# Layer 0's attention by head pairs instead of by halves: both halves' scores, then both halves' values, and all softmax sums through DRAM

## The chip, the cores and the metric

The kernel runs on one core of a Trainium2 chip. The metric is the device time of one launch in microseconds (us). A core has TensorE (PE in the profile; its weight loads are PEld), VectorE (DVE), ScalarE (ACT), GpSimd (POOL) and SyncE (SP, which issues DMAs). PSUM has eight banks, which hold the matmuls' results.

## The reference, cut to what matters

Eight images of 32×32 pixels with 384 channels go through two attention layers and a feed-forward network. What the change touches is layer 0's attention, with six heads of 64 channels and a position term:

```python
attn = einsum('bqd,bkd->bqk', q * SCALE, k)
attn = attn.reshape(b * NH, h, w, h, w) + rel_h[:, :, :, :, None] + rel_w[:, :, :, None, :]
attn = softmax(attn.reshape(b * NH, hw, hw), axis=-1)
out = einsum('bqk,bkd->bqd', attn, v)
...
x = x + (out @ proj_w + proj_b)
```

Each image has hw = 1024 tokens, so each head has 1024×1024 scores. Then follow layer 1 (one head of 384 channels, causal in blocks of 256 tokens) and, for five images, the feed-forward network.

## The kernel before, in words

**The images.** They run one after the other in the order 5, 0, 1, 2, 3, 4, 6, 7 (`ORDER`). An image's layer 0 is followed by its layer 1, and so on; products for the next image are placed among them. TensorE's order within the attention is fixed by hand: every matmul is issued after the one named in `last_matmul`. The other engines take their instructions in the order in which the program text issues them, unless `behind_of` or `tc.issue_after` puts one behind another. [...]

**The attention of one image** (`attend0_fast`). Six heads make three pairs p (`NPAIR`), 1024 queries make two halves of 512, 1024 keys make eight blocks c (`NJ`). A pair's two heads use the two halves of TensorE's rows or columns.

- `scores(p, c, half)`: for both heads, keys times queries (L904) and then the position term, a matmul of `unit` with the pair's table `r` (L908), into two PSUM banks. ScalarE takes the exponential of each (L915) into `pr`, 128 keys × (2 heads × 512 queries).
- `add_up`: VectorE adds the eight `pr` to `total`: one addition at L920, six at L922. These are the softmax sums over the blocks, still spread over 128 partitions.
- `values`: 32 passes (L930) of v against the eight `pr`, into one bank `av`. ScalarE copies it to `oT` (L1002).
- `over_tiles`: VectorE transposes the total within 32×32 blocks (L939) and reduces it (L941) to `few`, 128 × 32 numbers.
- `gathered`: SP writes `few` to DRAM (L949) and reads it back in four DMAs (L953) as `parts`, so that each partition has the four parts of its own sums. VectorE then reduces `parts` (L969).
- `reciprocals` with `parts=None`: instead of the DRAM trip TensorE multiplies `few` with `fold` (L964, `den`).
- `widened`: VectorE copies the reciprocals wide (L978) and transposes them (L979). The result scales `oT`: on GpSimd at L999, or on VectorE for an image's last halves (L1012, L1015).
- `later(p + 1)`, which calls `place`: rounds the next pair's position factors (ScalarE L784), subtracts to get the low part (two VectorE subtractions, L794), and sends both through 16 DMAs (L800; eight on SP's queue, eight on GpSimd's) into the `r` that L908 of the next pair reads.
- `residual`: SP loads the image x in four DMAs (L122), GpSimd adds the projection's bias in eight additions (L883). The result is first used when the projection is added.

**The order before.** For each pair and half: eight blocks of scores; the adds; behind the sixth of the seven adds (`adds[5]`) the reciprocals of the half before; the values. `residual` is placed in the first half of pair 1. `later` is placed after the first half of pairs 0 and 1. The sums of an image's last half go through L964. The projection (`pj`, L1021) then starts with tokens 0 to 511, in 24 passes: four token blocks j, three pairs i, two passes each.

**Buffers.** `page` has 12 buffers of 128×1024 floats (each `pr`, `total`, transposed total and wide takes one). `image` has ten larger buffers (q, k, v, `oT`, x, normalised forms, position factors). PSUM has eight banks in one pool.

**The end of the program.** The last image's output leaves in DMAs on SP's queue (L1525). Then a flag, set where a reciprocal or another value was unfit, is loaded, and a branch decides whether a general version of the whole program follows. It does not follow with these inputs.

Of the kernel before, what the change touches and what calls it, by code (L numbers as in the profile page):

```python
# [15 lines left out]
ALU = mybir.AluOpType  # L16
# [3 lines left out]
P = 128  # L20
B, H, W, C = 8, 32, 32, 384
T = H * W
NJ = T // P
NC = C // P
NH, HD = 6, 64
NPAIR = NH // 2
# [8 lines left out]
ORDER = (B_FFN, *range(B_FFN), *range(B_FFN + 1, B))  # L35
AFTER = dict(zip(ORDER, ORDER[1:]))
# [55 lines left out]
def conv_attn_hybrid(  # L92
# [19 lines left out]
    nc = tc.nc  # L112
# [15 lines left out]
    wproj_sb = tile_of("wproj_sb", [P, NC, C])  # L128
# [145 lines left out]
    N_SEEN = B * PER_IMAGE  # L274
    seen = const.tile([P, 2, N_SEEN], F32, name="seen")
    flag = const.tile([1, 1], I32, name="flag")

    def judge_sums(pools):

# [141 lines left out]
    def stages(pools):  # L421
# [98 lines left out]
        def project(w, cols, xT, j, name):  # L520

            ps = pools.o_tile(name)
            for k in range(NC):
                nc.tensor.matmul(ps[:, :C], xT[:, k, ts(j, P)], w[:, k, cols], start=(k == 0), stop=(k == NC - 1))  # L524
            return ps[:, :C]
# [361 lines left out]

        def attend0_fast(residual, b, q, k, r, v, later):


            oT = pools.image(f"oT_{b}")

            rows = (slice(0, HD), slice(HD, P))
            last_exp, last_matmul, last_few = [None], [None], [None]

            def behind_last():
                return tc.issue_after(last_matmul[0]) if last_matmul[0] is not None else contextlib.nullcontext()

            def scores(p, c, half):

                sc = [pools.o_tile(f"s0_{b}_{p}_{c}_{half}_{par}") for par in range(2)]
                with behind_last():
                    for par in range(2):
                        nc.tensor.matmul(  # L904
                            sc[par], k[rows[par], p, ts(c, P)], q[rows[par], p, ts(half, 512)], start=True, stop=False
                        )
                    for par in range(2):
                        last_matmul[0] = nc.tensor.matmul(  # L908
                            sc[par], unit[rows[par], c // 2 % 2].rearrange("i h w -> i (h w)"),
                            r(2 * (c // 4) + c % 2, p)[rows[par], ts(half, 512)], start=False, stop=True,  # L910
                        ).ins
                pr = pools.page(f"pr0_{b}_{p}_{c}_{half}")
                for par in range(2):
                    with behind_of(exp_loaded[0]):
                        last_exp[0] = nc.scalar.activation(pr[:, ts(par, 512)], sc[par], AF.Exp).ins  # L915
                return pr
# [58 lines left out]
            def widened(p, half, rt):  # L975
                room = pools.page(f"wide0_{b}_{p}_{half}")
                wide, rb = room[:, :512], room[:, 512:]
                nc.vector.tensor_copy(wide.rearrange("p (n i) -> p n i", i=32), rt.unsqueeze(2).to_broadcast([P, 16, 32]))  # L978
                nc.vector.transpose(rb, wide)  # L979
                return rb  # L980

            xt, waiting = None, None
            for p, half in itertools.product(range(NPAIR), range(2)):
                t, last = ts(half, 512), (p, half) == (NPAIR - 1, 1)
                prs = [scores(p, c, half) for c in range(NJ)]
                if b == ORDER[0] and (p, half) == (0, 0):
                    with tc.issue_after(last_row[0]):
                        layer1_forms(pools, raw1[0], 1)
                if b == ORDER[0] and (p, half) == (2, 0):
                    signs.append(binarize(pools))  # L990
                    next(signs[0])
                total, adds = add_up(p, half, prs)
                if waiting is not None:
                    p0, t0 = waiting[0], ts(waiting[1], 512)
                    with tc.issue_after(adds[4 if last else 5]):
                        rt = reciprocals(*waiting)
                    if not last:
                        rb = widened(p0, waiting[1], rt)
                        nc.gpsimd.tensor_tensor(oT[:, p0, t0], oT[:, p0, t0], rb, ALU.mult)  # L999
                av = values(p, half, prs)  # L1000
                if not last:
                    nc.scalar.copy(oT[:, p, t], av)  # L1002
                if (p, half) == (1, 0):
                    xt = residual()
                if half == 0 and p + 1 < NPAIR:
                    later(p + 1, last_exp[0], adds[-1])
                few = over_tiles(p, half, total)
                at_once = last or (b == ORDER[0] and p == NPAIR - 1)
                if last:
                    with tc.issue_after(last_few[0]):  # L1010
                        rb = widened(p0, waiting[1], rt)
                    nc.vector.tensor_tensor(oT[:, p0, t0], oT[:, p0, t0], rb, ALU.mult)  # L1012
                waiting = (p, half, few, None if at_once else gathered(p, half, few))
            rb = widened(p, half, reciprocals(*waiting))
            nc.vector.tensor_tensor(oT[:, p, t], av, rb, ALU.mult)  # L1015
            with behind_last():
                begun = {j: pools.o_tile(f"pj_{b}_{j}")[:, :C] for j in range(4)}
# [4 lines left out]
                                begun[j], oT[:, i, ts(j, P)], wproj_sb[:, i, :], start=(i == 0), stop=(i == NC - 1)  # L1022
                            ).ins

            def begin(j):
                begun[j] = project(wproj_sb, slice(0, C), oT, j, f"pj_{b}_{j}")

            def more(j):
                nc.vector.tensor_tensor(xt[:, j, :], begun[j], xt[:, j, :], ALU.add)

            return xt, (begin, more)

        def attend0_general(residual, b, q, k, r, v, later):
            state = {}
# [151 lines left out]
        def attend1_fast(xt, b, q, xT, v, other, start):  # L1186
# [24 lines left out]
            def products(av, j, cs, what):  # L1211
                for c in cs:
                    made = nc.tensor.matmul(av, prs[c][:, ts(j - c, P)], what(c), start=(c == 0), stop=(c == j)).ins  # L1213
                return made
# [5 lines left out]
            def add(j, av):  # L1220
                return nc.vector.scalar_tensor_tensor(
                    xt[:, j, :], av[:, :C], rt[:, j : j + 1], xt[:, j, :], ALU.mult, ALU.add
                ).ins
# [13 lines left out]
            def values_and_flag(j, av7):  # L1237
                av = pools.o_tile(f"av1_{b}_{j}")
                last = products(av[:, :C], j, range(j), lambda c: v[:, c, :C])
                worst, made = judge_sums(pools)  # L1240
                with tc.issue_after(made):
                    add(NJ - 1, av7)
                with tc.issue_after(last):
                    last = judge(pools, worst)
                with tc.issue_after(last):
                    products(av[:, :C], j, (j,), lambda c: v[:, c, :C])
                add(j, av)

            held = None if b in AFTER else 3
# [191 lines left out]
        def run(pools):  # L1441
# [49 lines left out]
            for b in ORDER:  # L1491
                xt, more = layer0(b, gn)

                def between():

                    if b in AFTER:
                        norm = group_norm_T(AFTER[b])
                        with behind_of(queries_ended[0]):
                            made = next(norm)
                        yield made  # L1500
                        for i in range(2):
                            with behind_of(last_score[0]):
                                next(norm, None)
                            yield
                        if pools.fast:
                            xf[AFTER[b]] = image_forms(AFTER[b], made, nc.gpsimd)

                started = []

                def start(gn):  # L1510

                    if b < B_FFN and not started:
                        started.append(ffn(xt, b, gn))
                        next(started[0])

                gn = attention1(xt, more, b, between, start)
                start(gn)
                add = next(started[0]) if started else None

                def finish(*js, b=b, xt=xt, add=add):  # L1520
                    if add:
                        xt = add(js)
                    dst = out[b].rearrange("(j p) c -> p j c", p=P)
                    for j in js[::2]:
                        (nc.gpsimd if b in AFTER else nc.sync).dma_start(  # L1525
                            out=dst[:, j : j + 2, :], in_=xt[:, j : j + 2, :]
                        )

                if b < B_FFN:
                    unfinished.append(finish)  # L1530
                else:
                    finish(*(range(NJ) if b in AFTER else (0, 1, 4, 5, 6, 7, 2, 3)))
# [3 lines left out]
    with ExitStack() as scope:  # L1536
        pools = Pools(scope, tc, "f")
        stages(pools)
    failed = nc.values_load(flag[0:1, 0:1], min_val=0, max_val=P)
    with tc.If(failed > 0), ExitStack() as scope:  # L1540
        stages(Pools(scope, tc, "g"))


# [36 lines left out]
```

## Time and profile before

| what | value |
|---|---|
| median of 3 runs | 2262.02 us (2261.88 to 2262.11) |
| the profiled execution | 2262.38 us, span 2260.7 us |
| granted TensorE clock, mean | 0.999 of full speed |
| TensorE busy | 2251.2 us |
| VectorE busy | 1613.0 us (71%) |
| ScalarE busy | 1208.5 us (53%) |
| GpSimd busy | 526.9 us (23%) |
| L904, L908, L930 (scores, position, values), busy | 399.0, 307.7, 340.2 us |
| L920 and L922 (adds), busy | 63.6 and 366.6 us |
| L915 (exponentials), busy | 412.5 us |

A profiled execution gives a span and, for each engine, the time in which it worked. A line of the timeline reads: start and duration in us, engine, line of the program, operation, output `<-` inputs, shape, number of instructions, and in brackets how long the engine had been idle before and what ended that. A pair of matmuls that overlap is counted in both, so a group's busy time can exceed the time that it takes on the clock. The chain of waits follows the work that ended last back to its start.

### The profile page before, as it was taken

To read this page: it belongs to the slowest core of one execution; us is meant where nothing else is said; L and a number is where in the kernel's file an instruction comes from. 1 tells how busy PE (TensorE), PEld (TensorE's weight loads), DVE (VectorE), ACT (ScalarE), POOL (GpSimd) and SP (SyncE) were. 2 spreads that over 40 slices of the span, in tenths; PEclk is the share of its full clock that TensorE was granted. 3 is DMA by queue.
4 is the path that set the end of the run, shared out by engine and by line. 5 is a ranking of instruction groups with operands and counts; after the bars stand their busy time and mean duration, and the time that the engine had idled before them with its cause. 6 is when DMAs were issued, how large, how long until landed. Compare 5 with 4: busy or idle time off the path is not lost.

```text
span 2260.7 us, 30149 instructions
## 1 busy us (share of the span) xinstructions
PE 2251.2 (100%) x10597; PEld 1380.3 (61%) x10597; DVE 1613.0 (71%) x2746; ACT 1208.5 (53%) x2181; POOL 526.9 (23%) x696
## 2 busy tenths in 40 slices
PE   9999999999999999999999999999999999999998
PEld 4547554768546677547685475874477754755475
DVE  6888578876788548886468884578854778727882
ACT  4654266337664457654477543767444766317541
POOL 7513231230231301313102313013040131221310
PEclk9999999999999999999999999999999999999999
DMA  7520562130730205520318203064102382016200
GB/s 188 158 86 29 162 138 68 49 148 29 155 100 29 84 29 126 129 58 1 112 39 189 56 29 112 24 148 112 30 9 104 71 173 64 7 47 155 55 1 30
DMA packets 182049, 188.50 MB, mean 83 GB/s; under 512 B 138764, under 2 KB 151489, under 8 KB 179073
## 3 DMA queue, kind: packets, MB, share of 16 engines
q1 hardware_dynamic: 163680, 115.80, 21.1%
q0 software_dynamic: 17376, 69.30, 9.8%
q8 instruction: 87, 1.43, 0.3%
q10 hardware_dynamic: 832, 1.38, 0.2%
q14 instruction: 74, 0.60, 0.1%
HBM read 84.52 MB, written 51.56 MB: 60 GB/s over the span
## 4 chain that ended last, share of the span: by engine, by line
PE 99%; DMA 0%; DVE 0%; SPq 0%; issue 0%
PE f_s L904 15%; PE f_av L930 15%; PE f_av L1213 8%; PE f_s L1199 8%; PE f_y L1407 7%; PE f_y L1357 7%; PE f_qk L578 6%; PE f_s L908 4%; PE f_pr_A L578 4%; PE f_pr_B L578 3%; PE f_pj L1021 3%; PE f_pj L524 3%; PE f_rel L578 2%; PE f_pr_1v_A L578 2%; PE f_pr_1q_A L578 2%; PE f_pr_1v_B L578 2%
## 5 line engine op out<-in xcount | busy, mean ns | idle before, releaser
L915 ACT ACTIVATE f_pr<-f_s 128x512 f32<-128x512 f32 x768 | 412.5, 595 | 41.8 <-PE f_s L908 37.1
L904 PE MATMUL f_s<-f_q,f_k 64*128 64x512 f32 x1536 | 399.0, 595 | 0.0
L922 DVE TENSOR_TENSOR f_sum<-f_sum,f_pr 128x1024 f32<-128x1024 f32 x288 | 366.6, 1273 | 25.9
L930 PE MATMUL f_av<-f_pr,f_v 128*64 128x512 f32 x1536 | 340.2, 595 | 0.0
L908 PE MATMUL f_s<-f_r,unit 64*128 64x512 f32 x768 | 307.7, 792 | 0.0
L930 PEld LDWEIGHTS f_av<-f_pr,f_v 128*64 128x64 f32 x1536 | 106.0, 137 | 218.2 <-issue 191.9
L904 PEld LDWEIGHTS f_s<-f_q,f_k 64*128 64x128 f32 x1536 | 145.6, 186 | 124.4 <-issue 66.2
L1199 PE MATMUL f_s<-f_q,f_lnT 128*128 128x512 f32 (+3 forms) x576 | 198.3, 488 | 0.0
L1213 PE MATMUL f_av<-f_v,f_pr 128*128 128x385 f32 (+1 forms) x576 | 195.4, 486 | 0.0
L800 POOL DMA_DIRECT2D f_r<-f_far x192 | 102.0, 534 | 382.0 <-DVE f_far L794 174.4
L1208 ACT ACTIVATE f_pr<-f_s 128x512 f32<-128x512 f32 (+3 forms) x96 | 47.0, 490 | 203.2 <-DVE f_s L1204 160.3
L1213 PEld LDWEIGHTS f_av<-f_v,f_pr 128*128 128x128 f32 x576 | 108.1, 190 | 77.0 <-issue 11.5
L1199 PEld LDWEIGHTS f_s<-f_q,f_lnT 128*128 128x128 f32 x576 | 100.7, 190 | 70.0 <-issue 46.9
L1368 DVE TENSOR_REDUCE am<-f_h 128x1 f32<-128x1024 f32 (+2 forms) x80 | 71.6, 946 | 95.6 <-ACT f_h L1361 95.6
L1361 ACT ACTIVATE f_h<-f_y,biases 128x256 f32<-128x256 f32 x240 | 100.6, 470 | 67.0 <-PE f_y L1357 67.0
L908 PEld LDWEIGHTS f_s<-f_r,unit 64*128 64x128 f32 x768 | 75.0, 187 | 89.9 <-issue 89.4
L578 PE MATMUL f_qk<-f_gnT,wq_sb 128*128 128x512 f32 x288 | 127.9, 595 | 0.0
L1407 PE MATMUL f_y<-f_w2a,f_hilo 128*128 128x384 f32 x640 | 127.2, 341 | 0.0
L1002 ACT COPY f_oT<-f_av 128x512 f32<-128x512 f32 x40 | 23.4, 585 | 190.2 <-PE f_av L930 190.2
L920 DVE TENSOR_TENSOR f_sum<-f_pr,f_pr 128x1024 f32<-128x1024 f32 x48 | 63.6, 1325 | 73.5 <-ACT f_pr L915 73.5
L1407 PEld LDWEIGHTS f_y<-f_w2a,f_hilo 128*128 128x128 f32 x640 | 112.6, 188 | 3.8 <-issue 1.4
L1311 POOL PARTITION_ALL_REDUCE qa<-qg x10 | 3.7, 365 | 459.1 <-DVE qg L1309 459.1
(286 smaller groups left out, 4154.4 us busy)
## 6 DMA issues: line engine op xcount, KB each, us to landing
f_far<-f_far SPq DMA_DIRECT2D x48, 512.0 KB, 5.3
f_r<-f_far SPq DMA_DIRECT2D x192, 128.0 KB, 3.3
f_r<-f_far POOLq DMA_DIRECT2D x192, 128.0 KB, 4.5
f_far<-f_far SPq DMA_DIRECT2D x192, 64.0 KB, 4.6
f_x<-in_x SPq DMA_DIRECT2D x32, 384.0 KB, 4.9
f_gnT<-in_xT SPq DMA_DIRECT2D x21, 512.0 KB, 4.7
f_w1a<-w1s POOLq DMA_DIRECT2D x5, 1536.0 KB, 6.7
f_w2a<-w2s POOLq DMA_DIRECT2D x5, 1536.0 KB, 7.3
```

Of the source, the lines that this page charges most:

```text
L578: last_product[0] = nc.tensor.matmul(*args, **kw).ins
L800: put = (nc.gpsimd if i else nc.sync).dma_start(out=r(part, p).bitcast(F32).rearrange("(m i) t -> i m t", i=4)[2 * i + d], in_=pages[i][ts ...
L904: nc.tensor.matmul(sc[par], k[rows[par], p, ts(c, P)], q[rows[par], p, ts(half, 512)], start=True, stop=False)
L908: last_matmul[0] = nc.tensor.matmul(sc[par], unit[rows[par], c // 2 % 2].rearrange("i h w -> i (h w)"), r(2 * (c // 4) + c % 2, p)[rows[pa ...
L915: last_exp[0] = nc.scalar.activation(pr[:, ts(par, 512)], sc[par], AF.Exp).ins
L922: adds.append(nc.vector.tensor_tensor(total, total, pr, ALU.add).ins)
L930: last_matmul[0] = nc.tensor.matmul(av[ts(par, HD), :], v[:, c, ts(2 * p + par, HD)], pr[:, ts(par, 512)], start=(c == 0), stop=(c == NJ - 1),
L1199: last_score[0] = nc.tensor.matmul(sc[:, lo:], xT[:, c // 4, k, ts(c % 4, P)], q[:, half, k, lo:], start=(k == 0), stop=(k == NC - 1),).ins
L1213: made = nc.tensor.matmul(av, prs[c][:, ts(j - c, P)], what(c), start=(c == 0), stop=(c == j)).ins
L1357: nc.tensor.matmul(ps, w1k[i // 2][:, ts(m, P)], xs[i % 2][:, half, i // 2, :], start=(i == 0), stop=(i == 2 * NC - 1))
L1361: nc.scalar.activation(pairs[i][:, m, :, :], ps[:, ts(i % 2, 256)].rearrange("p (j q) -> p j q", j=2), AF.Identity, bias=b1_sb[:, m : m + 1],)
L1407: nc.tensor.matmul(ps[:, :C], h, w, start=(i == 0), stop=(i == len(products) - 1))
```

## The change

It applies to seven of the eight images, all but the first in `ORDER`. The order of one of these images becomes, for each pair:

- the scores of half 0, whose last six exponentials go to two large `image` buffers (three in each) and whose first two go to pages;
- the reciprocals and widening of both halves of the pair before, and their products on GpSimd; `behind_of(last_wide[0])` puts the first add of this pair behind the last widening;
- the adds of half 0; the scores of half 1; the adds of half 1;
- in the last pair, `residual`;
- the values of half 0 and of half 1, each followed by its copy to `oT`;
- `later(p + 1)`, now behind the last add of half 1;
- both halves' transposes and reductions, each followed by its trip through DRAM, in the last pair too, so the matmul of L964 is not used.

After the last pair come the reciprocals of both halves and their products on VectorE, and then the projection in the order j = 0 to 3, each with i = 0, 1, 2. `oT` is taken from its pool after the first values of the image rather than at the start.

At the end of the program the flag is loaded before the last layer 1 addition, and the last output DMA goes to ScalarE's queue instead of SP's.

```diff
-            def scores(p, c, half):
+            def scores(p, c, half, pr=None):
...
-                pr = pools.page(f"pr0_{b}_{p}_{c}_{half}")
+                pr = pools.page(f"pr0_{b}_{p}_{c}_{half}") if pr is None else pr
...
-                nc.vector.transpose(rb, wide)
+                last_wide[0] = nc.vector.transpose(rb, wide).ins
                 return rb
+
+            def by_pairs():
+
+                oT, waiting = None, []
+                for p in range(NPAIR):
+                    last = p == NPAIR - 1
+                    rooms = [pools.flat(f"pr0_{b}_{p}_{i}") for i in range(2)]
+                    prs = [[scores(p, c, 0, rooms[(c - 2) // 3][:, ts((c - 2) % 3, T)] if c > 1 else None) for c in range(NJ)]]
+                    for p0, half, few, parts in waiting:
+                        with behind_of(last_few[0]):
+                            rb = widened(p0, half, reciprocals(p0, half, few, parts))
+                        t = ts(half, 512)
+                        nc.gpsimd.tensor_tensor(oT[:, p0, t], oT[:, p0, t], rb, ALU.mult)
+                    waiting = []
+                    with behind_of(last_wide[0]):
+                        sums = [add_up(p, 0, prs[0])]
+                    prs.append([scores(p, c, 1) for c in range(NJ)])
+                    sums.append(add_up(p, 1, prs[1]))
+                    if last:
+                        xt = residual()
+                    for half in range(2):
+                        av = values(p, half, prs[half])
+                        if oT is None:
+                            oT = pools.image(f"oT_{b}")
+                        if not (last and half):
+                            nc.scalar.copy(oT[:, p, ts(half, 512)], av)
+                    if not last:
+                        later(p + 1, last_exp[0], sums[1][1][-1])
+                    for half in range(2):
+                        with behind_of(last_few[0] if half else sums[1][1][-1]):
+                            few = over_tiles(p, half, sums[half][0])
+                        waiting.append((p, half, few, gathered(p, half, few)))
+                with behind_of(last_few[0]):
+                    for p, half, few, parts in waiting:
+                        t = ts(half, 512)
+                        rb = widened(p, half, reciprocals(p, half, few, parts))
+                        nc.vector.tensor_tensor(oT[:, p, t], av if half else oT[:, p, t], rb, ALU.mult)
+                begun = {}
+                with behind_last():
+                    for j in range(4):
+                        begun[j] = pools.o_tile(f"pj_{b}_{j}")[:, :C]
+                        for i in range(NC):
...
+            if b != ORDER[0]:
+                return rest_of(*by_pairs())
...
+                failed.append(nc.values_load(flag[0:1, 0:1], min_val=0, max_val=P))
                 add(j, av)
...
-                            (nc.gpsimd if b in AFTER else nc.sync).dma_start(
+                            (nc.gpsimd if b in AFTER else nc.scalar if j == js[-2] else nc.sync).dma_start(
...
-    failed = nc.values_load(flag[0:1, 0:1], min_val=0, max_val=P)
-    with tc.If(failed > 0), ExitStack() as scope:
+    with tc.If(failed[0] > 0), ExitStack() as scope:
```

More of the change, by code (lines that the diff above doesn't have):

```diff
@@ L276, in conv_attn_hybrid @@
     flag = const.tile([1, 1], I32, name="flag")
+    failed = []
     def judge_sums(pools):
@@ L888, in attend0_fast @@
         def attend0_fast(residual, b, q, k, r, v, later):
-            oT = pools.image(f"oT_{b}")
             rows = (slice(0, HD), slice(HD, P))
-            last_exp, last_matmul, last_few = [None], [None], [None]
+            last_exp, last_matmul, last_few, last_wide = [None], [None], [None], [None]
             def behind_last():
                 return tc.issue_after(last_matmul[0]) if last_matmul[0] is not None else contextlib.nullcontext()
-            def scores(p, c, half):
+            def scores(p, c, half, pr=None):
                 sc = [pools.o_tile(f"s0_{b}_{p}_{c}_{half}_{par}") for par in range(2)]
@@ L978, in widened @@
                 nc.vector.tensor_copy(wide.rearrange("p (n i) -> p n i", i=32), rt.unsqueeze(2).to_broadcast([P, 16, 32]))
-                nc.vector.transpose(rb, wide)
+                last_wide[0] = nc.vector.transpose(rb, wide).ins
                 return rb
+            def by_pairs():
[38 more added lines that the diff above has]
+                        for i in range(NC):
+                            with tc.issue_after(last_matmul[0]):
+                                last_matmul[0] = nc.tensor.matmul(
+                                    begun[j], oT[:, i, ts(j, P)], wproj_sb[:, i, :], start=(i == 0), stop=(i == NC - 1)
+                                ).ins
+                return xt, oT, begun
@@ L982, in attend0_fast, with rest_of, begin, more @@
+            def rest_of(xt, oT, begun):
+                def begin(j):
+                    begun[j] = project(wproj_sb, slice(0, C), oT, j, f"pj_{b}_{j}")
+                def more(j):
+                    nc.vector.tensor_tensor(xt[:, j, :], begun[j], xt[:, j, :], ALU.add)
+                return xt, (begin, more)
+            if b != ORDER[0]:
+                return rest_of(*by_pairs())
+            oT = pools.image(f"oT_{b}")
             xt, waiting = None, None
@@ L985, in attend0_fast @@
                 prs = [scores(p, c, half) for c in range(NJ)]
-                if b == ORDER[0] and (p, half) == (0, 0):
+                if (p, half) == (0, 0):
                     with tc.issue_after(last_row[0]):
                         layer1_forms(pools, raw1[0], 1)
-                if b == ORDER[0] and (p, half) == (2, 0):
+                if (p, half) == (2, 0):
                     signs.append(binarize(pools))
@@ L1007, in attend0_fast @@
                 few = over_tiles(p, half, total)
-                at_once = last or (b == ORDER[0] and p == NPAIR - 1)
+                at_once = last or p == NPAIR - 1
                 if last:
@@ L1023, in attend0_fast @@
                             ).ins
[L1025 to L1031, printed above, removed]
+            return rest_of(xt, oT, begun)
         def attend0_general(residual, b, q, k, r, v, later):
```

## The prediction

> **What bounds the kernel now.** I read the engine totals first, then the chain of work that ended last.
>
> ```profile
> PE 2251.2 (100%) x10597; PEld 1380.3 (61%) x10597; DVE 1613.0 (71%) x2746; ACT 1208.5 (53%) x2181; POOL 526.9 (23%) x696
> PE 99%; DMA 0%; DVE 0%; SPq 0%; issue 0%
> ```
>
> TensorE works 2251.2 of 2260.7 us and is the whole chain: only fewer or denser matmuls gain, and any wait put on TensorE costs its full length. Second, TensorE's timeline of one image (its attention begins at 606.30; I call that S):
>
> ```profile
> 647.12 7.09 PE L930 MATMUL f_av<-f_pr,f_v 128*64 128x512 f32 x32
> 654.14 1.13 PE L904 MATMUL f_s<-f_q,f_k 64*128 64x512 f32 x4
> 655.34 1.02 PE L904 MATMUL f_s<-f_q,f_k 64*128 64x512 f32 x4
> 656.42 1.02 PE L904 MATMUL f_s<-f_q,f_k 64*128 64x512 f32 x4
> 701.88 0.24 PE L964 MATMUL f_den<-few,fold 128*64 128x16 f32 x4
> 702.06 8.01 PE L1021 MATMUL f_pj<-wproj_sb,f_oT 128*128 128x384 f32 x24
> ```
>
> Eight key blocks of scores, then 32 value matmuls. The second block follows the first by 1.20 us, the third after 1.08: a change of kind costs about 0.1. L1021 begins at S+95.8, with no wait.
>
> Third, VectorE in the same image, because the change's text puts more in one row there:
>
> ```profile
> 609.90 1.23 DVE L920 TENSOR_TENSOR f_sum<-f_pr,f_pr 128x1024 f32<-128x1024 f32 x1 [2.10 <-ACT f_pr L915]
> 611.23 7.88 DVE L922 TENSOR_TENSOR f_sum<-f_sum,f_pr 128x1024 f32<-128x1024 f32 x6
> 619.02 3.16 DVE L794 TENSOR_TENSOR f_far<-f_far 64x1024 fp32r<-64x1024 f32 x2
> 622.22 1.25 DVE L939 STREAM_TRANSPOSE f_tr<-f_sum 128x1024 f32<-128x1024 f32 x1
> 623.50 1.22 DVE L941 TENSOR_REDUCE few<-f_tr 128x32 f32<-128x1024 f32 x1
> 625.85 1.23 DVE L920 TENSOR_TENSOR f_sum<-f_pr,f_pr 128x1024 f32<-128x1024 f32 x1 [1.14 <-ACT f_pr L915]
> ```
>
> VectorE starts 3.60 us after S, its seven adds take 9.12 us though blocks come each 1.09, and it idles only 1.1 us before the next half. In S to S+95.6 it is busy 81.6: slack of 14 us an image, and the change spends it.
>
> Fourth, the sums' way through DRAM (SP's issues) and what runs beside:
>
> ```profile
> 659.29 0.35 SPq L949 DMA_DIRECT2D f_few<-few  x1
> 662.58 2.02 SPq L953 DMA_DIRECT2D parts<-f_few  x4
> 671.94 0.34 SPq L949 DMA_DIRECT2D f_few<-few  x1
> 673.38 1.73 SPq L953 DMA_DIRECT2D parts<-f_few  x4
> ```
>
> From write to read it takes 3.3 us while POOL's copies of r (L800) are in flight, and 1.44 otherwise. Then 1.73 for four reads, which land 1.8 after issue (median).
>
> **What the Trainium skill says.** *DMA: Bandwidth & Descriptors*, "Issuing engines are not separate DMA queues": DMAs of scalar, sync and gpsimd share the same 16 engines. The 3.3 against 1.44 us agrees. *GPSIMD Engine Reference*, "1. Specifications": GpSimd shares SBUF interfaces with VectorE, so they contend in two-input operations. The trace agrees: beside POOL's x additions (L883) an L922 add takes 1.84 us instead of 1.23, the addition 1.97 instead of 0.99. *TensorE: Matmul & The Clock Gate*, "Part 1: The HAM clock gate": after about 3.4 us of idleness TensorE runs at half clock until it has been busy as long. The trace shows the second part: the first matmuls, 1.53 to 7.0, run at 0.85 us spacing instead of 0.43.
>
> **The change, part by part.** It concerns seven of eight images.
>
> *Gain on TensorE.* Two halves' scores follow each other, then two halves' values. A half's scores take 8.93 us against 8×1.09 = 8.72, its values 7.02 against 8×0.858 = 6.86: one pair saves 0.36, 21 pairs 7.6 us. The den matmul L964 of the last half goes: 701.88 to 702.06, 0.18×7 = 1.3. So 8.9 us, 1.27 an image. A pair is then 31.53 us long and L1021 could begin at S+94.3; its first i=2 matmul, which needs oT of pair 2 half 0, at S+95.6.
>
> *End of the program.* The flag is read earlier (before the last add) and the last output DMA goes to ScalarE's queue. Before, SP issues its output at 2254.03 and the flag load at 2254.45, and joins at 2258.42; but VectorE leaves at 2258.41. SP gets about 1.7 shorter, VectorE nothing: I take −1.1, bounds 0 and −2. The earlier load may also make an engine wait for the flag's last write: 0 to 1, in the bounds.
>
> *ScalarE, buffers.* The exponentials are as many; two take 0.99 against TensorE's 1.09 a block, so 16 in a row hold. Six blocks of half 0 go to two image buffers, which in pair 0 held the image before's output (sent over 20 us earlier) and in pair 1 r's sources (copied out by S+34.8, first needed S'+6.8 = 38.3). Zero; the cover is 3.5 us, and if it goes ScalarE is late next.
>
> *VectorE, one row now.* For each pair: 14 adds (2×9.12 = 18.24), lo (L794, 3.19), two transposes and reductions (2.50 and 2.44, together 4.94), two trips through DRAM, then the two reciprocals and widenings (1.76 each, up to the transpose's end) **before** the next pair's first add. Before, those stood behind the sixth add, where the trip was hidden. The adds now wait for DRAM, and everything queued behind (14 adds, lo, both sums) with them. Relative to S:
>
> - Pair 0: adds 3.6 to 21.84, lo to 25.03 (16 r copies on SP and POOL go out then), sums ready at 27.5 and 30.0. First trip, slowed by those copies: reads issue from 27.5+3.3 = 30.8, land at 34.2, the second half's at 36.0. Two items: pair 1's adds start at 37.7, not at the 35.1 (S'+3.6) that the exponentials allow. r for pair 1 lands near 29.8, needed at 32.1: zero, slack 2.3.
> - Pair 1: POOL's product (L999) beside an add costs 0.88 (2.11 instead of 1.23): adds end 56.8, lo 60.0, POOL's copies of r land 60.3+4.5 = 64.8. L908 of pair 2 needs them at 63.6: **TensorE waits 1.2**. First sum 62.5, adds of pair 2 at 72.7 (again 10.2 from sum to add).
> - Pair 2: x loads and POOL's eight additions of x now fall here (before, in pair 1), beside the adds: eight times 0.61 = 4.9. Adds end 72.7+18.24+0.88+4.9 = 96.7. No lo now. Sum 99.2, trip undisturbed 4.5 → 103.8; reciprocal, widening 1.76 and product 0.7 → 106.3.
> - TensorE needs that at 95.6. **Total wait 10.8 an image** (1.2 + 9.6).
>
> The second piece exceeds 3.4 us, so the projection restarts at half clock: estimate 1.7 (half of 3.4, from the page) to 2.7 (5.5/2, trace); I take 2.0. The second half's oT follows 1.8 to 2.5 after the first; L1021's j 0 to 3 (8.0 us) read half 0 only and half 1 is first read at j=4, so it costs zero, with 5 us of cover. oT's copies on ScalarE end with the values: zero. SP's queue carries, in order, both sums' writes before the eight reads in pairs 0 and 1 (a read waits for its own write only): inside the trips above.
>
> Sum: (10.8+2.0−1.27)×7 = 80.7; with the end −1.1: about +79.6 on the profiled execution's 2262.4 (span 2260.7 and 1.7 around it), which is 0.4 above the median of 2262.02. **Prediction 2341 us.** What a measurement of this kernel can tell from no change is about 0.2%, 4.5 us.
>
> **Rivals.**
>
> - *VectorE keeps up* (faster): the trip hides and only the denser order counts: 2262.4−8.9−1.1 = 2252. For it: 14 us of idle VectorE in each image. Against: those gaps lie at the starts of halves, and with quick trips (sum to add 8.3) and no cost of x additions the last sum still stands at 90.5, oT at 90.5+4.5+2.5 = 97.5, 1.9 after need.
> - *Half of the row's excess* (slower): no trip is slowed by r's copies and x additions cost the adds half (2.4): oT at 97.5+2.4 (rival above), wait 4.3, clock loss half of 1.7: net (4.3+0.9−1.27)×7 = 27.5 → 2289. For: trips of 1.44 are there in the trace; against: those were the ones with no r copies in flight.
> - *Worse* (slower): each trip slow, the last too (+1.9), and clock loss 2.7: net (12.7+2.7−1.27)×7 = 99 → 2360.
> - *Buffers wait too* (slower): the exponentials of pair 1 stand for an image buffer whose r copies are late; from 3.5 us of lateness on, TensorE's half-1 scores stop on PSUM. Alone at 3 an image: 2252+21 = 2273; with the row it is hidden by VectorE's lateness.
> - *The change does not do what it says*: the order of the row could have been resolved otherwise by the scheduler; the program's order on VectorE has den before the first add, so 0.02.
>
> The other side, with its point: the change is faster when the wait is below 1.27 an image, i.e. if the row from the first add of pair 0 to oT of pair 2 takes under 93.3 instead of 102.7 us.
>
> **Numbers.** Main 0.62; half 0.15; worse 0.10; buffers alone 0.03; VectorE keeps up 0.07 (not-as-said within it); near zero, between these, 0.03. Range: main's unknowns (0.7 us either way for each of three trips and the clock, all together 2.8×7: ±20) and the neighbours: 2286 to 2363. Faster 0.07, same 0.03, slower 0.90.
>
> **What would show it.** In the profile after: TensorE's share falls to about 97%, the chain gets VectorE and DMA shares; the first L1021 i=2 matmul waits about 9.6 us for VectorE's oT in each of seven images, and the clock record dips there; L908 of pair 2 waits about 1 for r; L920 of pairs 1 and 2 begins at S'+6 and S''+8, idle before it put down to the parts DMA; the mean of L922 rises from 1273 ns to about 1350. Wrong if TensorE has no gap at the projection, if the adds of pair 1 begin by S'+4, or if the gap stands at the exponentials instead.

## The result, and the profile after

The changed kernel takes 2380.41 us (median of 4, 2374.89 to 2382.93) against 2262.04 for the kernel before: a ratio of 1.052, interval 1.0502 to 1.0539. It is slower, as forecast, but by 118 us and not by 79; the prediction's range ended at 2363. The profiled execution took 2379.8 us with a span of 2378.1.

The page of the kernel after, totals and the chain of waits:

```profile
PE 2275.9 (96%) x10569; PEld 1400.9 (59%) x10569; DVE 1677.3 (71%) x2753; ACT 1210.7 (51%) x2181; POOL 570.1 (24%) x696
...
PE 82%; DVE 11%; DMA 2%; issue 2%; SPq 1%; ACT 1%; DVEq 0%; POOL 0%; ACTq 0%; POOLq 0%
...
L920 DVE TENSOR_TENSOR f_sum<-f_sum,f_pr 128x1024 f32<-128x1024 f32 x288 | 394.7, 1372 | 42.6 <-ACT f_pr L913 13.9
```

TensorE is 96% busy and no longer the whole chain: VectorE and DMAs stand in it. A VectorE add (L922 before, L920 now) has gone from 1273 to 1372 ns. TensorE's waits in the kernel after (engine, what waited, for what: us in total, times, the longest):

```profile
PE f_pj L1022 <- DVE f_oT L1015: 82.9, 7, 12.9
PE f_s L906 <- issue: 6.4, 12, 2.0
PE f_s L902 <- ACT f_pr L913: 2.9, 7, 0.7
```

Seven waits of 11.8 us on average at the projection, for VectorE's product, where before there was none. The second line is the wait for the position tables r (the profile names no releaser; in the built program it is the landing of r's copies). The third, waits for exponentials, all lies in image 0; the prediction's sum had it at zero.

I use S again for the start of an image's attention. From one S to the next (for the last image, to the end), image 0 (second in the order) takes 28.8 us more than before, the six others 14.6, 15.0, 15.6, 15.0, 15.5 and 13.4. That is 117.9 in all; the first image starts 0.5 us earlier than before, and the span is 117.4 longer. The stretch after the last of the projection's 24 passes is as long as before in every image within 0.4 us, the program's end included. The whole difference lies inside the attention and its projection.

VectorE in image 1 of the kernel after (S = 634.68):

```profile
661.00 1.22 DVE L939 TENSOR_REDUCE few<-f_tr 128x32 f32<-128x1024 f32 x1
...
670.05 0.26 DVE L967 TENSOR_REDUCE den<-parts 128x16 f32<-128x64 f32 x1 [5.43 <-DMA parts<-f_few]
...
670.72 0.42 DVE L976 COPY f_wide<-rt 128x512 f32<-128x512 f32 x1
...
672.46 1.13 DVE L976 COPY f_wide<-rt 128x512 f32<-128x512 f32 x1
...
674.25 1.18 DVE L918 TENSOR_TENSOR f_sum<-f_pr,f_pr 128x1024 f32<-128x1024 f32 x1
...
724.87 9.10 DVE L920 TENSOR_TENSOR f_sum<-f_sum,f_pr 128x1024 f32<-128x1024 f32 x6
...
741.02 0.26 DVE L967 TENSOR_REDUCE den<-parts 128x16 f32<-128x64 f32 x1 [2.23 <-DMA parts<-f_few]
...
742.94 0.69 DVE L1015 TENSOR_TENSOR f_oT<-f_oT,f_wide 128x512 f32<-128x512 f32 x1
```

The first sum of pair 0 is ready at 662.2. VectorE then idles until its parts come back from DRAM at 670.05, and only at 674.25, S+39.6, does pair 1's first add begin. The last product ends at 743.6. SP's queue shows how the sums go to DRAM and come back, first for pair 1 (first sum ready at 699.08), then for pair 2 (736.38):

```profile
699.11 2.75 SPq L947 DMA_DIRECT2D f_few<-few  x2
701.95 3.96 SPq L951 DMA_DIRECT2D parts<-f_few  x8
...
736.40 0.34 SPq L947 DMA_DIRECT2D f_few<-few  x1
737.84 1.75 SPq L951 DMA_DIRECT2D parts<-f_few  x4
```

In pair 2 the first read follows its write after 1.44 us. In pair 1 both writes stand ahead of all reads, and the second write waits for the second sum (701.49). The first read goes out 2.84 us after its write, just behind the second write, in this as in all seven images. TensorE, same image:

```profile
730.56 1.56 PE L1022 MATMUL f_pj<-wproj_sb,f_oT 128*128 128x384 f32 x4
743.68 9.31 PE L1022 MATMUL f_pj<-wproj_sb,f_oT 128*128 128x384 f32 x20 [11.56 <-DVE f_oT L1015]
```

Four matmuls with pairs 0 and 1, then 11.56 us of nothing, then the other twenty. Those take 9.31 us where 24 took 8.01 before. The granted clock in the profile is 0.50 of full speed from 736 to 748.9 us and 1.00 after 749.2: the passes restarted at the low clock.

### The profile page after: what moved, and what is told of

The parts are those of the page before. It is cut to its first block, busy times and chain, and to the rows that moved or that the text cites. A ratio compares the mean times of both kernels' runs of the same rounds, so it can differ in the third digit from the quotient of the medians.

```text
span 2378.1 us, 30131 instructions
## 1 busy us (share of the span) xinstructions
PE 2275.9 (96%) x10569; PEld 1400.9 (59%) x10569; DVE 1677.3 (71%) x2753; ACT 1210.7 (51%) x2181; POOL 570.1 (24%) x696
## 4 chain that ended last, share of the span: by engine, by line
PE 82%; DVE 11%; DMA 2%; issue 2%; SPq 1%; ACT 1%; DVEq 0%; POOL 0%; ACTq 0%; POOLq 0%
PE f_s L902 10%; PE f_av L1267 8%; PE f_s L1253 8%; PE f_y L1462 7%; PE f_y L1412 7%; DVE f_sum L920 6%; PE f_av L928 6%; PE f_qk L579 5%; PE f_pr_A L579 4%; PE f_s L906 3%; PE f_pr_B L579 3%; PE f_pj L1022 3%; PE f_pj L525 3%; PE f_rel L579 2%; PE f_pr_1v_A L579 2%
## 5 line engine op out<-in xcount | busy, mean ns | idle before, releaser
L920 DVE TENSOR_TENSOR f_sum<-f_sum,f_pr 128x1024 f32<-128x1024 f32 x288 | 394.7, 1372 | 42.6 <-ACT f_pr L913 13.9
L902 PE MATMUL f_s<-f_q,f_k 64*128 64x512 f32 x1536 | 408.5, 600 | 2.9 <-ACT f_pr L913 2.9
L906 PE MATMUL f_s<-f_r,unit 64*128 64x512 f32 x768 | 312.8, 790 | 6.4 <-issue 6.4
L902 PEld LDWEIGHTS f_s<-f_q,f_k 64*128 64x128 f32 x1536 | 155.9, 188 | 113.0 <-ACT f_pr L913 71.4
L1022 PE MATMUL f_pj<-wproj_sb,f_oT 128*128 128x384 f32 x168 | 74.2, 603 | 82.9 <-DVE f_oT L1015 82.9
L1267 PEld LDWEIGHTS f_av<-f_v,f_pr 128*128 128x128 f32 x576 | 108.2, 190 | 77.0 <-issue 11.5
L488 ACT ACTIVATE lsd<-lsd 128x4 f32<-128x4 f32 x26 | 5.4, 207 | 265.6 <-DVE lsd L486 265.5
L906 PEld LDWEIGHTS f_s<-f_r,unit 64*128 64x128 f32 x768 | 80.3, 189 | 102.0 <-issue 100.7
L884 POOL TENSOR_TENSOR f_x<-f_x,pb 128x384 f32<-128x384 f32 x64 | 116.6, 1856 | 0.0
```

Of the source, the lines that this page charges most:

```text
L884: nc.gpsimd.tensor_tensor(xt[:, j, :], xt[:, j, :], pb, ALU.add)
L902: nc.tensor.matmul(sc[par], k[rows[par], p, ts(c, P)], q[rows[par], p, ts(half, 512)], start=True, stop=False)
L906: last_matmul[0] = nc.tensor.matmul(sc[par], unit[rows[par], c // 2 % 2].rearrange("i h w -> i (h w)"), r(2 * (c // 4) + c % 2, p)[rows[pa ...
L920: adds.append(nc.vector.tensor_tensor(total, total, pr, ALU.add).ins)
L1022: last_matmul[0] = nc.tensor.matmul(begun[j], oT[:, i, ts(j, P)], wproj_sb[:, i, :], start=(i == 0), stop=(i == NC - 1)).ins
```

## The experiments

**1. The program's end alone** (layer 0 as before):

```diff
+                failed.append(nc.values_load(flag[0:1, 0:1], min_val=0, max_val=P))
                 add(j, av)
...
-    failed = nc.values_load(flag[0:1, 0:1], min_val=0, max_val=P)
...
-(nc.gpsimd if b in AFTER else nc.sync)
+(nc.gpsimd if b in AFTER else nc.scalar if j == js[-2] else nc.sync)
```

> Only the program's end is changed: the flag is loaded before the last layer 1 addition and the last output leaves on ScalarE's queue; layer 0 is as before. Theory from the two traces (the stretch from the last projection pass to the end is 92.57 us before and after): no gain, 2262.0 +-0.4. Rival, the step of the prediction: SP's end gets shorter and 1.1 us are gained, 2260.9; and if the earlier load delays the last addition, up to 2263.

Measured: 2261.51 against 2261.92, ratio 0.9998 (0.9989 to 1.0007). No difference can be told; the prediction's gain of 1.1 us is not shown.

**2. Image 0 in the order of before:**

```diff
-            if b != ORDER[0]:
+            if b not in ORDER[:2]:
                 return rest_of(*by_pairs())
```

(The rest of the edit gives the old order back the conditions by which it tells the first image from the others.)

> The changed kernel, but image 0 (the second in order, the first that runs by pairs) keeps the order of before. In the changed kernel's trace this image loses 28.8 us and the six others 13.4 to 15.6 each, 89.0 together. Theory: the 28.8 belong to this image's own buffers (its second large buffer of pair 1 comes free only when the last position matmul of the pair has read it, so its exponentials stand behind half 1's and hold six PSUM banks): the six others stay as they are, 2262+89 = 2351. Rival: the cost belongs to whichever image is the first by pairs; then image 1 takes it over, 2262+28.8+5x14.8 = 2365.

Measured: 2350.27, ratio 1.0383 (1.0366 to 1.0401), 30 us less than the change. Image 1 does not take the cost over: it is 320.3 us long, as before the edit. The excess is image 0's own. TensorE and VectorE in that image's pair 1, in the kernel after, TensorE first:

```profile
340.47 1.02 PE L902 MATMUL f_s<-f_q,f_k 64*128 64x512 f32 x3
...
344.71 1.18 PE L902 MATMUL f_s<-f_q,f_k 64*128 64x512 f32 x3 [0.46 <-ACT f_pr L913]
...
347.02 1.18 PE L902 MATMUL f_s<-f_q,f_k 64*128 64x512 f32 x3 [0.47 <-ACT f_pr L913]
...
352.58 2.07 PE L902 MATMUL f_s<-f_q,f_k 64*128 64x512 f32 x3 [0.27 <-ACT f_pr L913]
...
355.83 2.07 PE L902 MATMUL f_s<-f_q,f_k 64*128 64x512 f32 x3 [0.27 <-ACT f_pr L913]
```

```profile
348.70 1.23 DVE L920 TENSOR_TENSOR f_sum<-f_sum,f_pr 128x1024 f32<-128x1024 f32 x1
363.35 3.50 DVE L920 TENSOR_TENSOR f_sum<-f_sum,f_pr 128x1024 f32<-128x1024 f32 x3 [13.42 <-ACT f_pr L913]
```

Half 1's blocks come each 2.3 us and then, at half clock, each 3.25, instead of 1.09; and VectorE stands 13.4 us for an exponential, though exponentials of half 1 go on ending in the meantime: it keeps to its order. ScalarE's record in this pair is ten exponentials at the usual pace, then fourteen in twos as TensorE's blocks come, then the last eight together, from 361.75 on. The built program gives the reason. In this image the second large buffer of pair 1 is the one that holds r for this very pair, free only after the pair's last L906. So ScalarE's order has the exponentials of half 0's blocks 5 to 7 behind all but the very last of half 1's. Six of eight PSUM banks stay taken, and TensorE and ScalarE pass the last two to and fro. Pair 2 starts at S+76.6 instead of S+63.0: 13.6 us. In the other images that buffer had held the position factors, whose copies had landed. That the cost is image 0's is shown by this run; that it is this buffer is read from the program and fits the order in the trace, but no run gave image 0 another buffer.

All later runs but experiment 8 keep image 0 in the old order, so they compare with 2350.27.

**3. The sums almost without adds** in the six images by pairs:

```diff
-                for pr in prs[2:]:
+                for pr in prs[2:2] if b not in ORDER[:2] else prs[2:]:
```

> As second_old, and in the six images by pairs each half's sum adds only the first two of its eight blocks (six of the seven additions are left out, so the softmax sums are not the reference's). Theory: VectorE's row (14 adds a pair, sums, trip, reciprocals, then the next adds) is what makes TensorE wait; without 12 of 14 adds it ends before S+92, nothing waits, and only the denser order is left: six images gain 1.48 each, 2262-8.9 = 2253. Rival, the trip through DRAM or the buffers hold TensorE whatever the adds cost: the wait at the projection stays over 5 us an image, 2295 or more.

Measured: 2254.48, ratio 0.9968 (0.9957 to 0.998). TensorE has no wait left in the attention, projections begin at S+94.6, the images take 304.2 to 304.6 us instead of 305.7. That is the gain of the denser order by itself, 7.4 us for six images with the end's edit in it; and it shows that VectorE's row, not the order, the buffers or the trip as such, makes TensorE wait.

**4. The reciprocals behind the sixth add:**

```diff
-                    for p0, half, few, parts in waiting:
-                        with behind_of(last_few[0]):
+                    with behind_of(last_few[0]):
+                        sums = [add_up(p, 0, prs[0])]
+                    for p0, half, few, parts in waiting:
+                        with behind_of(sums[0][1][5]):
                             rb = widened(p0, half, reciprocals(p0, half, few, parts))
...
-                    with behind_of(last_wide[0]):
-                        sums = [add_up(p, 0, prs[0])]
```

> As second_old, and the reciprocals and widenings of the pair before stand behind the sixth add of the pair (as in the kernel before) and no longer ahead of its first add; the trips through DRAM of pairs 0 and 1 are then covered by adds. Theory A, the row is full of VectorE's own work: pair 1's adds start at S+35.1 instead of 39.6, pair 2's at about 68 instead of 75, the last sum at 98.6, reciprocals' product at 105.9 instead of 109.0: 3 us an image less, 2351-19 = 2332. Rival B, the adds' wait for DRAM is nearly all of it: two waits of 6.5 us go, the projection's wait falls under 3 us without clock loss, 2351-6x11 = 2285 or less.

Measured: 2324.29, ratio 1.0277 (1.026 to 1.0294): 26 us less, nearer to A (2332) than to B (2285 or less). TensorE's waits for r fall as well, from 7.5 us in six images to 1.2, which A had not counted. Half 0's last sum stands at S+98.2, and the projection waits 8.7 us (52.4 in six images) in place of 11.6 (69.4 in six, experiment 2). The trips' waits in pairs 0 and 1 are a part of the row's length; with them covered, VectorE's own work still ends late.

**5. Pair 2's sums through TensorE:**

```diff
-                        waiting.append((p, half, few, gathered(p, half, few)))
+                        waiting.append((p, half, few, None if last else gathered(p, half, few)))
```

> As second_old, and both halves of pair 2 get their sums through TensorE (the den matmul of before) instead of the trip through DRAM. Theory, one row on VectorE: the last trip (first sum to its reduction, 4.6 us in the changed kernel's image 1) goes, the wait at the projection falls by 4.3: 2350-6x4.3 = 2324. Rival, the den matmul waits on TensorE as long as the trip took, because the row's adds are what is late: 2350-6 or no change.

Measured: 2331.6, ratio 1.0314 (1.0298 to 1.033): 18.7 us less, where 26 were expected. The projection starts late as a whole here, at S+105, because the two den matmuls, which wait for the sums, stand ahead of its first passes. The last trip costs, but its place on TensorE gives part of the gain back.

**6. Without GpSimd's bias additions to x:**

```diff
-                for j in range(NJ):
+                for j in range(NJ if b in ORDER[:2] else 0):
                     nc.gpsimd.tensor_tensor(xt[:, j, :], xt[:, j, :], pb, ALU.add)
```

> As second_old, and GpSimd's eight additions of the projection's bias to x are left out in the six images by pairs (the output lacks that bias there); the loads of x stay. In the changed kernel the 14 adds of pair 2 take 24.3 us where those of pair 0 take 18.3. Theory, GpSimd's additions stretch VectorE's adds: they take 19.2, all later steps move up by 5, 2350-6x5 = 2320. Rival, the adds are long for another reason (DMA traffic of x, reciprocals' products): 2350-6x1 or no change.

Measured: 2322.93, ratio 1.0267 (1.0252 to 1.0283): 27.3 us less, 4.6 an image. The group of adds in this run:

```profile
L920 DVE TENSOR_TENSOR f_sum<-f_sum,f_pr 128x1024 f32<-128x1024 f32 x288 | 370.9, 1288 | 30.0 <-DVE f_sum L920 1.4
```

1288 ns, against 1366 in experiment 2 and 1273 in the kernel before. The 4.9 us that the prediction took for this contention are about right.

**7. Every such wait taken out** (4 and 5 together, `later` behind half 0's adds, x loaded on ScalarE's queue only behind half 0's last copy, the projection in its old order):

```diff
+                    if not last:
+                        later(p + 1, last_exp[0], sums[0][1][-1])
                     prs.append([scores(p, c, 1) for c in range(NJ)])
...
-                    if last:
-                        xt = residual()
...
+                        if last and not half:
+                            with tc.issue_after(copied):
+                                xt = residual(nc.scalar)
```

> As second_old with every wait that the runs so far point to taken out of VectorE's row: reciprocals of the pair before behind the sixth add, the position factors' subtraction behind half 0's adds, den on TensorE in pair 2, x loaded on ScalarE's queue only after half 0's copy in pair 2 so that GpSimd's additions fall behind the adds, projection's order as before. Theory, the row then is bound by when the exponentials of a pair come and by VectorE's own work: 66.6+18.3+5.1+5.0+2.5 = 97.5 for the product that the projection wants at about 96.5, so the denser matmuls' gain is just eaten: 0 to +0.5 us an image, 2262 to 2265. Rival 1, a wait of several us is left somewhere: over 2275. Rival 2, the order by pairs gains as soon as VectorE isn't late: 2262-6x1.2 = 2255.

Measured: 2276.92, ratio 1.0067 (1.0052 to 1.0083): 12 us over the upper end of what I expected, and in the first rival's region: a wait was left. ScalarE, in the first of the six images:

```profile
607.22 8.67 ACT L913 ACTIVATE f_pr<-f_s 128x512 f32<-128x512 f32 x16 [1.08 <-PE f_s L906]
615.77 3.10 ACT L785 CAST f_far<-f_far 64x1024 fp32r<-64x1024 f32 x2
618.90 6.48 ACT L913 ACTIVATE f_pr<-f_s 128x512 f32<-128x512 f32 x13
```

I had thought that two rounding copies between the halves' exponentials would be made up. They take 3.10 us, PSUM fills, and pair 1 begins at S+32.7 instead of S+31.5, pair 2 at S+65.5 instead of S+63.0.

**8. Only pair 0 by pairs** (seven images; pairs 1 and 2 as before):

```diff
-            oT = pools.image(f"oT_{b}")
+            oT, waiting = first_pair() if b != ORDER[0] else (pools.image(f"oT_{b}"), [])
...
+                if b != ORDER[0] and p == 0:
+                    continue
```

> Only pair 0 of seven images is run with both scores and then both values (six exponentials in two large buffers); its reciprocals stand behind the sixth add of pair 1; pairs 1 and 2 are as before, the end of the program as in the changed kernel. Theory: VectorE has room in pair 0 (adds end at S+21.9, sums at 30.0, next adds only at 35.1), nothing waits, and each image gains one change of order, 0.36 to 0.5 us: 2261.5-7x0.4 = 2258.7. Rival: the sums of two halves arriving late shift pair 1's row beside the x additions, the last sum comes later than S+95.1 and the projection waits: 2265 or more.

Measured: 2261.74, ratio 1.0 (0.9992 to 1.0008): nothing. TensorE's pair 1 begins 0.4 earlier, but in six of the seven images the last sum comes at S+95.3 to 96.0 instead of 95.1, and the projection with it (waits for `few` at the den matmul, 2.1 us in all). Even one pair's gain is spent on VectorE's row.

**9. As 7, with the rounding behind half 1's exponentials:**

```diff
-                    if not last:
-                        later(p + 1, last_exp[0], sums[0][1][-1])
                     prs.append([scores(p, c, 1) for c in range(NJ)])
...
+                    if not last:
+                        later(p + 1, last_exp[0], sums[1][1][2])
```

> As pairs_best, with one step elsewhere: the rounding of the next pair's position factors on ScalarE stands behind half 1's exponentials, not between the two halves' (and the subtraction behind half 1's third add). In pairs_best pair 1 begins at S+32.7 and pair 2 at S+65.5 instead of 31.5 and 63.0: 2.4 us an image, with TensorE waiting for exponentials. Theory: that is the two rounding copies (each about 1 us) ahead of half 1's exponentials; the 2.4 go, 2277-6x2.4 = 2262.5, and nothing is gained on the kernel before since den of half 1 waits for the second sum ahead of the projection. Rival: the 2.4 are VectorE's subtraction or buffers held longer; no change, 2275 or more.

Measured: 2262.78, ratio 1.0003 (0.9994 to 1.0011): the 2.4 us an image are gone, and the time is the kernel before's. The edit moves VectorE's subtraction along with ScalarE's rounding, so the two are not parted by a run; the 3.10 us between the exponentials in experiment 7 speak for the rounding. The projection begins at S+94.8 and then waits about 1 us for the product.

**10. As 9, with half 1's den matmul inside the projection:**

```diff
+                settle(*waiting[0])
+                for at, (j, ks) in enumerate(((0, (0, 1)), (1, (0, 1)), (2, (0, 1)), (0, (2,)), (1, (2,)), (2, (2,)), (3, (0, 1, 2)))):
+                    if at == 3:
+                        settle(*waiting[1])
```

(`settle` is the reciprocals, the widening and the product of one half.)

> As pairs_round, and the den matmul of half 1 in pair 2 stands on TensorE behind the projection's first i=0, 1 matmuls of j = 0 to 2, so that the projection starts when the values end (S+94.5). VectorE's row must then give half 0's product by S+98.4; by its durations it gives it at 97.4. Theory: no wait is left and the denser matmuls pay, six images x (1.27-0.18) and the end's 0.4: 2261.9-6.9 = 2255. Rival: contention of GpSimd's additions with the last steps of VectorE's row makes it 1 us late again: 2260 to 2262.

Measured: 2258.04 (21 runs, 2257.49 to 2259.10) against 2261.86 (33 runs, none below 2261.55), ratio 0.9984 (0.9977 to 0.999). TensorE's projection in this run's image 1, the first by pairs, and then VectorE's product of half 0 in it:

```profile
700.17 0.24 PE L962 MATMUL f_den<-few,fold 128*64 128x16 f32 x4
700.35 4.14 PE L1029 MATMUL f_pj<-wproj_sb,f_oT 128*128 128x384 f32 x12
704.41 0.29 PE L962 MATMUL f_den<-few,fold 128*64 128x16 f32 x4
704.64 4.14 PE L1029 MATMUL f_pj<-wproj_sb,f_oT 128*128 128x384 f32 x12
```

```profile
702.84 1.52 DVE L1018 TENSOR_TENSOR f_oT<-f_oT,f_wide 128x512 f32<-128x512 f32 x1
```

VectorE's product ends at 704.36, just before TensorE wants it at 704.64, and nothing waits. This version beats both kernels, the one before by 0.2%. It gains 3.8 us and not the 6.9 expected. Images take 304.9 to 305.3 us where experiment 3 had 304.2 to 304.6: the two den matmuls account for some 0.4 of that, and in the profiled execution one image started 1.4 us late for r; how much of the rest each takes was not separated.

## Why the prediction was right or wrong

**Right: the bound, the row and its direction.** The table sets the prediction's steps beside image 1 of the kernel after, us from S:

| step | predicted | measured |
|---|---|---|
| first sum of pair 0 | 27.5 | 27.5 |
| first parts back | 34.2 | 35.4 |
| adds of pair 1 begin | 37.7 | 39.6 |
| adds of pair 1 end | 56.8 | 58.7 |
| wait for r in pair 2 | 1.2 | 1.3 |
| adds of pair 2 begin | 72.7 | 75.0 |
| adds of pair 2 end | 96.7 | 99.3 |
| parts back | 103.8 | 106.3 |
| projection goes on | 106.3 | 109.0 |

Experiments 3, 4, 5 and 6 each take one piece out of this row and the wait shrinks with it. *VectorE keeps up* falls; *half of the row's excess* falls too: L920's mean rose to 1372 ns, and experiment 6 gave back 4.6 of the 4.9.

The mechanism held. What failed are two sizes in the sum: the buffers' zero in image 0, and the length of the row in every image.

**Wrong, first term: image 0.** The step "Zero; the cover is 3.5 us" for the buffers was read from the images with a steady predecessor and taken for all seven. Image 0 lost 28.8 us, 17.3 more than the 11.5 forecast for an image. Of that, 13.6 are the exponentials placed behind half 1's; the rest, 3.7, is near what the other images lost beyond the forecast (3.3 each). My rival *Buffers wait too* had the mechanism (scores stop on PSUM) but for the wrong reason, a late copy of r, and at 3 us an image.

**Wrong, second term: the first stretch from sum to add.** I took 10.2 us; image 1 has 12.0 (27.5 to 39.6): the trip 7.8 instead of 6.7, and the two reciprocals with widenings 4.2 instead of 3.5, because the second widening copy stands beside GpSimd's product of the first and takes 1.13 instead of 0.42. The second such stretch came to 10.6. I had priced GpSimd's product only beside an add. The row ends 2.7 later; over six images the excess is 89.1−6×11.53 = 19.9 us. About 2.5 of it are the low clock (2.4 us on the mean of these images, 2.0 forecast), the rest is the later row. The step "a read waits for its own write only" was wrong for the queue too: in pair 1 the first read stood behind the second half's write, 2.84 us after its own write, where pair 2 needed 1.44. No run put the reads ahead of that write.

**Wrong, third term: the end.** −1.1 was put down, experiment 1 shows nothing that can be told from zero, inside the bounds given.

17.3, 19.9 and 1.1 are 38.3. The first image's earlier start takes 0.5 off, and that leaves the 37.8 us between the sum and the profiled 2379.8: 2262.4 + 79.6 is 2342.0, and the 2341 put down is a slip. A second slip is S+94.3 for the projection's start: three pairs of 31.53 are 94.6, which experiment 3 measured. The gain on TensorE was about right: 1.27 an image forecast, 1.1 to 1.5 in experiment 3. The low clock was right in kind and somewhat small: the twenty passes after the wait cost 2.1 to 2.8 us too much against 20/24 of the 8.01 before, 2.0 forecast.

The range failed for both reasons. Its upper end, *worse*, allowed 14.1 us an image (the last trip slow by 1.9, the clock by 0.7). The six images took 14.8 on the mean, and seven such images alone would have come to about 2366, past the range's 2363. Image 0 with its other order of buffers added 14 more.

## What to carry to other kernels

Grouping matmuls of one kind saves their changes, here 0.3 to 0.4 us a pair (experiment 3, without the den matmul's 0.18 us an image), but makes what the other engines get uneven: VectorE has nothing to add during 14 us of values and must then catch up. Before doing it, write down the second engine's row from first input to the product that the main engine wants, with every wait ahead of it, and see that it fits; then place what waits (a trip through DRAM, reciprocals, another engine's additions) behind work that can go on. And look at every image by itself: here one of seven lost twice as much as each of the others.

## What the runs showed of the hardware that I had not expected

TensorE's clock fell to half without a long gap. In image 0 of the kernel after, with blocks each 2.3 us and gaps of at most 0.66 us in the record, passes went from 0.59 to 1.06 us each after about 8 us of this; the granted clock is 1.00 from 340 to 349 us and 0.50 from 350 to 362. Being partly busy was enough here. The page that the prediction cites (the Trainium skill, *TensorE: Matmul & The Clock Gate*, Part 1) names an idle window of about 3.4 us; further on in the same part, under "A second HAM failure mode: psum-queue depth-cycling", it tells of short idle times between groups of matmuls that make the clock swing, and this stretch agrees with that. Which share of busy time decides was not tried.

A VectorE copy of 512 elements with a single input (L976) takes 0.42 us alone. Where a GpSimd product was under way when it began, it took 0.75 to 1.20 us in the kernel after, and each of these thirteen copies ended 0.28 or 0.29 us after the product did. So in these records it is not slowed in proportion: it waits for the product's end. In the first image, whose order was not changed, one such copy began during a GpSimd bias addition and stood behind that and the six that followed, 6.75 us in all (from 94.57 us of the span on). The contention is not confined to adds with two inputs.
